# A four-layer graph network on one core: setup's weight products, the last group's transposes and the order of all steps are rewritten

## The chip, the core and the metric

The kernel runs on one core of a Trainium2 chip, in fp32 throughout. The metric is the time of one execution on the device in microseconds, the median of three runs. TensorE (PE) multiplies, VectorE (DVE), ScalarE (ACT) and GpSimd (POOL) do the element-wise work, and SyncE (SP) issues the DMAs.

## The reference

A batch of 128 elements, each with 128 nodes of 512 features, passes four layers that share one 128x128 adjacency matrix; each is followed by a residual and a layer norm.

```python
# layer 0: norm_adj = adj * rsqrt(deg) on both sides
x = LN(x + norm_adj @ (x @ W0) + bias)
# layer 1: W1 = W2 = adj, so C - A is the bias b and the maximum over the last axis stays elementwise
x = LN(x + max_m relu(A[n] + (C - A)[m]))
# layer 2
q, k, v = x @ Wq.T, x @ Wk.T, x @ Wv.T
rel = adj.T * (q @ k.T);  rel = rel / norm(rel, axis=2)
x = LN(x + rel @ v)
# layer 3
h = x @ W;  e = leaky_relu(h @ a1 [:, None] + h @ a2 [None, :]) * adj
x = LN(x + elu(softmax(e) @ h + beta * h))
```

## The kernel before

The batch is cut into 32 groups of four elements. A group passes a fixed chain of steps, and the chains of several groups overlap in time. A step's name has the group before the dot and the operation behind it (`4.z1`, `s.g0` for a step of setup).

The steps of a group, in the order of its data:
- `ld` loads x. `y` is norm_adj times x, which leaves x transposed. `w` is the product with W0 and `dw`, `uw`, `bi` add it and the bias to x (TensorE, then VectorE and POOL). `stw`, `vaw`, `pow`, `nbw`, `apw` are statistics, variance, power -1/2, shift and the normalising pass on ScalarE.
- `xt` and `xd` transpose x: VectorE transposes 32x32 squares into a tile `u`, of which there is one buffer, and sixteen DMAs on SyncE (L558) put the squares in place. `z` is x times Wq^T Wk, `v` is x times Wv^T, `r` is z times x transposed, one 128x128 block per element. `rm` multiplies by the adjacency, `sq` and `rp` make the norm, `rt`, `wr`, `cr` transpose the result (`relT`) by VectorE's squares and DMAs through DRAM. `f` is `relT` times v, `fa` adds it, and `stv` to `apv` normalise.
- `nt`, `nd` transpose again as `xt`, `xd` do. `k` is the product with W, `sc` makes the two row products s1, s2 (eight VectorE operations), `pw`, `pe` write s2 to DRAM and read it back spread over all partitions, `pl`, `ej`, `ei`, `ex`, `rd`, `so` are the leaky relu, the mask, the softmax and beta's diagonal, `at`, `aw`, `cat` transpose the attention (`attT`) through DRAM. `h` is attention times k, `em`, `ee`, `ea` are the elu with the residual, `stk` to `apk` normalise, `fin` stores.

The four large products w, z, v, k of a group are not computed as eight block products but as seven (class `Product`): both factors are cut in two by two blocks, sums of blocks are formed ahead (`sy`, `sx`, `sn` on POOL for the left factor, `w_sum`, L349, on VectorE for the weights), and seven products of four 256-wide matmuls each, numbered in the order `ORDER`, go to four PSUM banks. Product 6 accumulates onto the bank of product 1, 3 onto that of 5, 4 onto that of 7, each after the bank's first content was read:

```python
    ORDER = (1, 2, 5, 7, 6, 3, 4)
    ONTO = {6: 1, 3: 5, 4: 7}
```

For z, v and k the steps `c`, `d`, `t`, `u` copy and add the banks into a tile (ScalarE, VectorE, ScalarE, POOL). [...]

Setup computes, besides the normalised adjacency: Wq^T Wk in four row blocks of four 512-wide matmuls (`g`, L425) with copies on ScalarE (`cg`), Wv transposed by sixteen TensorE transposes (`t`, L440) with copies on ScalarE (`ct`), the sums of all weights (`s`, `sg`, `sv`), the products of W with a1 and a2 (`q`, eight VectorE operations), and eight TensorE transposes `wa` that spread these over all partitions.

Nothing is scheduled by a program at run time: the strings HEAD, TURN and TAIL list all steps, and each engine's queue holds its instructions in the order of that list. HEAD starts the first groups, TURN is repeated with one group more each time, TAIL ends. A step that waits holds up everything that is behind it on its engine. In TURN, TensorE's order is z of group g, f of g-1, r of g, w of g+1, y of g+2, v of g, h of g-2, k of g-1.

Of the kernel before, what the change touches and what calls it, by code (L numbers as in the profile page):

```python
# [37 lines left out]
F32 = mybir.dt.float32  # L38
# [6 lines left out]
TINY = 1.2e-38  # L45
GB = 4
# [15 lines left out]
s.t3 1.uw11 1.stw0 s.ct2 2.y10 s.ct3 1.stw1 2.y00 2.bi10 2.cy10 2.y11 2.cy00 s.sv0 2.y01 2.cy11
s.sv2 0.z1 s.sv1 2.cy01 s.sv3 1.stw2 0.sx0 0.z2 0.cz1 1.stw3 0.sx1 1.vaw 0.z5 0.dz2 0.sx2 0.z7
1.pow 0.cz5 0.sx3 0.z6 0.dz7 2.sy0 0.z3 0.tz 1.nbw 2.sy1 1.apw0 1.apw1 1.xt0 0.uz11 0.z4 1.apw2
0.dz3 2.sy2 1.xt1 1.apw3 0.r0 0.dz4 2.bi00 1.xt2 0.r1 1.xt3 0.r2 2.sy3 1.xd 0.r3 2.bi11 0.v1
0.rm 0.rt 0.sq0 2.bi01 0.sq1 0.v2 0.cv1 0.sq2 0.sq3 0.v5 0.rp 0.dv2 0.v7 0.cv5 0.v6 0.dv7 0.v3
0.tv 0.wr 0.uv11 0.v4 0.dv3 1.sx0 0.cr 3.y10 0.dv4 1.sx1 3.y00 3.cy10 3.y11 3.cy00 1.sx2 3.y01
3.cy11 3.sy1 3.w1 3.cy01 3.sy0 3.w2 3.dw1 1.sx3 3.w5 3.dw2 3.sy2 3.bi10 3.w7 3.dw5 3.sy3 3.w6
3.dw7 3.bi00 3.w3 3.bi11 3.tw 3.bi01 3.w4 3.uw10 3.dw3 0.f0 3.uw01 3.dw4 0.f1 0.fa0 3.uw11 0.f2
0.fa1 0.f3 0.stv0 1.z1 0.fa2 0.fa3 0.stv1 1.z2 1.cz1 0.stv2 0.stv3 1.z5 1.dz2 0.vav 3.stw0 0.pov  # L70
1.z7 1.cz5 3.stw1 0.nbv 1.z6 3.stw2 0.apv0 1.dz7 0.apv1 0.nt0 0.apv2 1.z3 3.stw3 1.tz 0.apv3
0.nt1 1.uz11 1.z4 1.dz3 0.nt2 0.nt3 2.w1 1.dz4 3.vaw 3.pow 2.w2 2.dw1 3.nbw 3.apw0 2.w5 2.dw2
3.apw1 3.apw2 2.w7 2.dw5 3.apw3 2.w6 2.dw7 2.w3 2.tw 2.uw01 2.w4 2.uw10 2.dw3 2.stw0 2.uw11 s.wa
0.nd 2.dw4 2.stw1 1.r0 2.stw2 2.stw3 1.r1 0.sc00 1.r2 2.vaw 1.r3 0.sc01 2.pow 0.sc10 1.v1 1.rm
2.nbw 1.sq0 1.rt 1.v2 1.cv1 0.sc11 2.apw0 0.sc20 2.apw1 1.v5 1.dv2 2.apw2 0.sc21 1.wr 2.apw3
1.v7 0.sc30 1.cv5 0.sc31 1.sq1 1.sq2 0.pw 1.v6 1.dv7 1.sq3 0.sn0 2.xt0 1.cr 2.xt1 1.v3 1.tv
0.sn1 2.xt2 2.xt3 0.sn2 1.v4 1.dv3 0.pe 1.uv11 0.k1 2.xd 1.dv4 0.sn3 0.k2 0.pl0 1.rp 0.ck1 0.pl1
0.pl2 0.k5 0.dk2 0.pl3 0.ej 0.ei 0.k7 0.ck5 0.ex0 0.ex1 0.k6 0.dk7 0.ex2 0.ex3 0.rd 0.so0 0.k3
0.tk 0.so1 0.so2 0.so3 0.uk11 0.at 0.k4 0.dk3 0.aw 1.f0 0.dk4 3.xt0 2.sx0 1.f1 1.fa0 0.cat 1.f2
2.sx1 3.xt1 1.f3 3.xt2 2.sx2 4.y10 3.xt3 1.fa1 4.y00 3.xd 4.cy10 4.bi10 1.fa2 4.y11 4.cy00 1.fa3  # L80
2.sx3 4.y01 4.cy11 1.stv0 2.z1 4.cy01 4.sy0 1.stv1 1.stv2 4.sy1 2.z2 2.cz1 1.stv3 4.sy2 1.vav
2.z5 2.dz2 1.pov 4.sy3 2.z7 2.cz5 1.nbv 4.bi00 1.apv0 2.z6 2.dz7 1.apv1 1.sc00 4.bi11 1.apv2
1.sc01 2.z3 2.tz 4.bi01 1.sc10 1.apv3 1.sc11 2.uz11 2.z4 2.dz3 1.nt0 3.sx0 2.r0 1.sc20 3.sx1
2.dz4 2.r1 1.nt1 2.r2 3.sx2 1.nt2 2.r3 1.nt3 3.sx3 2.v1 1.sc21 2.rm 1.sc30 2.sq0 2.v2 2.cv1 2.rt
2.sq1 1.sc31 2.wr 2.sq2 2.v5 2.sq3 2.dv2 1.pw 2.rp 2.v7 2.cv5 2.cr 2.v6 2.dv7 2.v3 1.pe 2.tv
2.uv11 2.v4 2.dv3 1.pl0 0.h0 1.nd 2.dv4 1.pl1 1.pl2 0.h1 0.em0 1.pl3 1.ej 0.h2 0.ee0 0.em1 0.h3
0.em2 0.ee1 3.z1 0.em3 0.ee2 0.ea0 0.ee3 0.ea1 3.z2 3.cz1 0.ea2 0.ea3 3.z5 0.stk0 0.stk1 3.z7
3.cz5 0.stk2 0.stk3 3.z6 3.dz7 0.vak 1.ei 0.pok 3.z3 3.tz 3.dz2 1.ex0 3.uz11 1.ex1 3.z4 1.ex2
0.nbk 3.dz3 1.sn0 0.apk0 0.apk1 0.fin0 4.w1 1.sn1 3.dz4 0.apk2 0.fin1 0.apk3 1.sn2 0.fin2 4.w2
4.dw1 1.ex3 0.fin3 1.sn3 1.rd 4.w5 1.so0 1.so1 1.so2 1.so3 4.w7 5.ld 4.dw5 1.at 4.dw2 1.aw 4.w6  # L90
4.dw7 4.w3 4.tw 4.uw01 1.cat 4.w4 4.uw10 4.dw3 4.stw0 4.uw11 2.f0 4.dw4 2.f1 2.fa0 4.stw1 2.f2
2.fa1 2.f3 2.fa2 1.k1 2.fa3 2.stv0 1.k2 1.ck1 2.stv1 2.stv2 1.k5 1.dk2 2.stv3 1.k7 1.ck5 4.stw2
2.vav 4.stw3 2.pov 1.k6 1.dk7 2.nbv 4.vaw 2.apv0 4.pow 1.k3 1.tk 2.nt0 2.apv1 1.uk11 1.k4 1.dk3
2.apv2 2.nt1 2.apv3 2.nt2 3.r0 1.dk4 3.r1 2.nt3 3.r2 4.nbw 2.nd 2.sc00 4.apw0 3.r3 2.sc01 4.apw1
1.h0 2.sc10 4.apw2 3.rm 1.h1 4.apw3 1.em0 3.sq0 1.h2 1.em1 3.sq1 1.h3 1.ee0 1.em2 1.ee1 3.v1
1.em3 1.ee2 3.rt 1.ee3 1.ea0 3.v2 3.sq2 1.ea1 3.cv1 3.sq3 1.ea2 3.rp 3.v5 1.ea3 1.stk0 3.wr
1.stk1 3.v7 3.cv5 1.stk2 1.stk3 3.v6 3.dv7 2.sn0 3.cr 4.xt0 3.v3 3.tv 2.sn1 1.vak 4.xt1 4.xt2
2.sn2 3.v4 4.xt3 3.dv2 1.pok 3.dv3 5.y10 4.xd 2.sn3 3.dv4 5.y00 5.cy10 1.nbk 5.y11 5.cy00 2.sc11
3.uv11 1.apk0 5.y01 2.sc20 5.sy1 1.apk1 2.sc21 2.k1 1.apk2 2.sc30 5.bi10 1.apk3 2.sc31 2.k2
2.ck1 5.bi00 5.cy01 5.cy11 2.k5 5.bi11 2.dk2 5.sy0 2.k7 2.ck5 5.bi01 1.fin0 2.k6 2.dk7 1.fin1  # L100
5.sy2 1.fin2 1.fin3 5.sy3 2.k3 2.tk 2.pw 4.sx0 2.k4 2.dk3 4.sx1 6.ld 4.z1 2.dk4 4.sx2 2.pe
2.uk11 4.z2 4.cz1 4.sx3 4.z5 4.dz2 2.pl0 2.pl1 2.pl2 4.z7 4.cz5 2.pl3 2.ej 4.z6 4.dz7 2.ei 4.z3
2.ex0 4.tz 2.ex1 4.uz11 4.z4 2.ex2 4.dz3 2.ex3 2.rd 2.so0 3.f0 4.dz4 3.f1 2.so1 3.fa0 3.f2 3.fa1
3.f3 3.fa2 4.r0 3.stv0 3.fa3 4.r1 3.stv1 4.r2 3.stv2 4.r3 3.stv3 5.w1 2.so2 3.vav 2.so3 4.rm
3.pov 5.w2 5.dw1 4.sq0 4.sq1 3.nbv 2.at 3.apv0 5.w5 5.dw2 2.aw 3.apv1 3.nt0 3.apv2 3.sc00 5.w7
3.apv3 5.dw5 4.sq2 3.nt1 4.sq3 2.cat 5.w6 5.dw7 4.rp 3.nt2 5.w3 3.nt3 5.tw 4.rt 5.uw01 3.nd
3.sc01 5.w4 5.uw10 5.dw3 3.sc10 5.uw11 6.y10 5.dw4 5.stw0 6.y00 6.cy10 6.bi10 5.stw1 6.y11
6.cy00 6.bi00 5.stw2 6.y01 6.cy11 5.stw3 4.v1 6.sy0 6.cy01 3.sc11 6.sy1 5.vaw 3.sc20 4.v2 4.cv1
3.sc21 5.pow 3.sc30 4.v5 6.sy2 4.wr 5.nbw 4.dv2 6.sy3 4.v7 5.apw0 3.sc31 4.cv5 6.bi11 5.apw1
5.xt0 3.pw 4.v6 4.dv7 5.apw2 4.cr 3.sn0 5.xt1 5.apw3 4.v3 5.xt2 4.tv 3.sn1 5.xt3 3.sn2 4.v4 3.pe  # L110
4.dv3 4.uv11 2.h0 5.xd 4.dv4 3.sn3 2.h1 2.em0 3.pl0 2.h2 2.em1 6.bi01 2.ee0 2.h3 2.ee1 2.em2
3.pl1 2.ea0 3.k1 2.ee2 2.em3 3.pl2 3.pl3 2.ea1 2.ee3 3.k2 2.ea2 3.ck1 2.ea3 2.stk0 3.k5 2.stk1
2.stk2 3.k7 3.ck5 2.stk3 3.ej 3.k6 2.vak 3.dk7 2.pok 3.ei 3.k3 3.tk 2.nbk 3.dk2 3.ex0 3.uk11
2.apk0 3.k4 3.dk3 2.apk1 5.sx0 2.fin0 2.apk2 2.fin1 5.sx1 5.z1 3.dk4 2.apk3 2.fin2 3.ex1 2.fin3
5.sx2 3.ex2 5.z2 5.cz1 5.sx3 3.ex3 3.rd 5.z5 5.dz2 7.ld 3.so0 3.so1 3.so2 5.z7 5.cz5 3.so3 3.at
3.aw 5.z6 5.dz7 5.z3 5.tz 5.uz11 3.cat 5.z4 5.dz3 4.f0 5.dz4 4.f1 4.fa0 4.f2 4.stv0 4.f3 4.fa1
4.fa2 5.r0 4.fa3 5.r1 4.stv1 5.r2 4.stv2 5.r3 4.stv3 6.w1 5.rm 4.vav 5.sq0 5.rt 4.pov 5.sq1 6.w2
6.dw1 5.wr 5.sq2 5.sq3 4.nbv 4.apv0 5.rp 6.w5 6.dw2 4.apv1 4.nt0 4.apv2 4.sc00 5.cr 6.w7 4.apv3
6.dw5 4.nt1 6.w6 6.dw7 4.nt2 4.nt3 6.w3 6.tw 4.sc01 4.nd 6.uw01 4.sc10 6.w4 6.uw10 4.sc11 6.dw3
6.uw11 7.y10 4.sc20 6.dw4 7.y00 7.cy10 7.bi10 6.stw0 7.y11 7.cy00 6.stw1 7.bi00 7.y01 7.cy11  # L120
6.stw2 5.v1 7.sy0 7.cy01 6.stw3 7.sy1 4.sc21 5.v2 5.cv1 6.vaw 4.sc30 6.pow 4.sc31 5.v5 7.sy2
# [58 lines left out]
TURN = """  # L180
# [87 lines left out]
def kernel(  # L268
# [116 lines left out]
    weights = {"0": (w0, w0_t), "g": (gq, gq_t), "v": (wvT, wvT_t), "3": (w3, w3_t)}  # L385
    W = {k: w_blocks(*v) for k, v in weights.items()}

    class Setup:


        def __init__(self):
# [12 lines left out]
        def root(self):  # L404
            nc.gpsimd.tensor_tensor(self.root_, self.safe, minus_half[:, 0:1], ALU.pow)
# [557 lines left out]
```

## Time and profile before

| | us |
|---|---|
| median of 3 runs | 2049.76 (2047.73 to 2051.08) |
| profiled execution | 2050.26 |
| its span, first to last instruction | 2048.5 |
| TensorE busy in the span | 2020.1 |
| VectorE busy | 1472.0 |
| POOL busy | 1006.9 |
| ScalarE busy | 771.8 |

Busy time is that of the profiled execution. The profiled execution took 1.8 us more than its span. A row such as `L595 PE MATMUL p_w<-w_t,S_y` names the line, the engine, the operation and the tiles; each fp32 matmul of 128x256 shows as two records. A matmul's record is longer than its distance to the next[...]: costs on TensorE are read from the starts of the records, not from their lengths.

### The profile page before, as it was taken

The page shows a single profiled execution, that of the slowest core. Times are in us where ns is not written, and L with a number is a line of the kernel's source. Part 1 is how long each engine was busy: PE and PEld are TensorE (multiplying, and loading weights), DVE is VectorE, ACT ScalarE, POOL GpSimd, SP SyncE. Part 2 cuts the span into 40 slices and gives each one's busy share as a digit, 9 for nine tenths or more (in the row PEclk, how much of TensorE's full clock was granted, in tenths as well). Part 3 has the DMA queues.
Part 4 walks back from the last instruction along what each step waited for, and adds up shares of the span by engine and source line. Part 5 has one row for each costly group of instructions (what it writes and reads, how often), then busy time and mean ns, then how long its engine had stood idle before and what let it go on. Part 6 is the DMA issues. An engine that isn't in the chain of part 4 may idle for free.

```text
span 2048.5 us, 29135 instructions
## 1 busy us (share of the span) xinstructions
PE 2020.1 (99%) x9786; PEld 1699.6 (83%) x9786; DVE 1472.0 (72%) x3048; ACT 771.8 (38%) x1609; POOL 1006.9 (49%) x840
## 2 busy tenths in 40 slices
PE   9999999999999999999999999999999999999996
PEld 6988888888888888888888888888888888888874
DVE  5477767677776777766776767777667767876876
ACT  2233334343333433343433334433334334332434
POOL 5735354554435555345545355554355452654432
PEclk9999999999999999999999999999999999999998
DMA  6224344433434433434434444334344333443533
GB/s 231 43 50 74 85 89 102 101 78 78 93 93 94 103 62 90 97 91 98 83 77 93 92 95 101 70 84 97 88 98 98 66 90 103 82 95 60 106 65 100
DMA packets 732980, 184.27 MB, mean 90 GB/s; under 512 B 684832, under 2 KB 684960, under 8 KB 732832
## 3 DMA queue, kind: packets, MB, share of 16 engines
q1 hardware_dynamic: 732832, 182.42, 41.2%
q8 instruction: 78, 1.28, 0.3%
q14 instruction: 70, 0.57, 0.1%
HBM read 64.82 MB, written 50.40 MB: 56 GB/s over the span
## 4 chain that ended last, share of the span: by engine, by line
PE 96%; SPq 1%; DVE 1%; issue 1%; DMA 1%; ACT 0%; POOL 0%; POOLq 0%; ACTq 0%; DVEq 0%
PE p_z L595 19%; PE p_w L595 19%; PE p_v L595 18%; PE p_k L595 17%; PE py L639 6%; PE pl_v L778 5%; PE pr L737 5%; PE pl_k L778 5%; SPq L558 1%; PE pg L425 1%; DVE prod L797 0%; SPq L572 0%; ACT x L699 0%; DMA s<-d_s 0%; DVE C_k L487 0%
## 5 line engine op out<-in xcount | busy, mean ns | idle before, releaser
L490 POOL TENSOR_TENSOR x<-x,t_w 128x512 f32<-128x512 f32 x96 | 119.5, 1273 | 158.5 <-ACT t_w L484 157.1
L487 DVE TENSOR_TENSOR x<-p_w,x 128x512 f32<-128x512 f32 x192 | 131.7, 687 | 81.0 <-PE p_w L595 66.8
L797 DVE SCALAR_TENSOR_TENSOR prod<-x,wa_bc 128x512 f32<-128x512 f32 x256 | 171.8, 671 | 4.6 <-ACT x L699 0.9
L595 PE MATMUL p_k<-w_t,S_n 128*128 128x256 f32 x768 | 171.5, 379 | 2.9 <-DVE C_k L487 1.9
L595 PE MATMUL p_w<-w_t,S_y 128*128 128x256 f32 x768 | 171.0, 379 | 0.0
L595 PE MATMUL p_z<-S_x,gq_t 128*128 128x256 f32 x768 | 171.0, 379 | 0.0
L595 PE MATMUL p_v<-wvT_t,S_x 128*128 128x256 f32 x768 | 171.0, 379 | 0.0
L490 POOL TENSOR_TENSOR x<-x,bias_bc 128x512 f32<-128x512 f32 x128 | 162.1, 1278 | 15.6 <-PE py L639 13.7
L595 PEld LDWEIGHTS p_k<-w_t,S_n 128*128 128x128 f32 x768 | 145.7, 190 | 23.8 <-DVE C_k L487 2.7
L595 PEld LDWEIGHTS p_w<-w_t,S_y 128*128 128x128 f32 x768 | 145.9, 190 | 19.8
L595 PEld LDWEIGHTS p_z<-S_x,gq_t 128*128 128x128 f32 x768 | 145.9, 190 | 19.8
L595 PEld LDWEIGHTS p_v<-wvT_t,S_x 128*128 128x128 f32 x768 | 145.9, 190 | 19.8
L494 POOL TENSOR_TENSOR r_v<-v,minus_half 128x4 f32<-128x4 f32 x32 | 32.9, 1029 | 255.9 <-DVE v L686 247.8
L753 ACT ACTIVATE sq<-rel 128x128 f32<-128x128 f32 x128 | 39.6, 309 | 267.0 <-DVE rel L487 264.3
L494 POOL TENSOR_TENSOR r_k<-v,minus_half 128x4 f32<-128x4 f32 x32 | 32.5, 1016 | 214.0 <-DVE v L686 211.4
L639 PEld LDWEIGHTS py<-nadjT,x 128*128 128x128 f32 x1024 | 121.5, 195 | 4.1 <-issue 1.4
L639 PE MATMUL py<-nadjT,x 128*128 128x128 f32 x1024 | 121.9, 278 | 0.4 <-DVE nadjT L418 0.4
L699 ACT ACTIVATE x<-x,nb,r_w 128x512 f32<-128x512 f32 x128 | 96.9, 808 | 66.8 <-DVE nb L693 62.2
L778 PE MATMUL pl_k<-C_k,attT 128*128 128x512 f32 x256 | 116.8, 599 | 3.7 <-DVE C_k L487 3.0
L778 PE MATMUL pl_v<-C_v,relT 128*128 128x512 f32 x256 | 116.7, 599 | 2.8 <-DMA relT<-d_r 2.8
L490 POOL TENSOR_TENSOR C_z<-C_z,t_z 128x512 f32<-128x512 f32 x32 | 40.6, 1270 | 160.2 <-ACT t_z L484 160.2
L487 DVE TENSOR_TENSOR C_z<-p_z,t_z 128x512 f32<-128x512 f32 x64 | 44.1, 688 | 91.2 <-PE p_z L595 88.2
(991 smaller groups left out, 4644.5 us busy)
## 6 DMA issues: line engine op xcount, KB each, us to landing
out_dram<-x SPq DMA_DIRECT2D x128, 256.0 KB, 2.1
x<-in_x_dram SPq DMA_DIRECT2D x31, 1024.0 KB, 5.4
d_r<-ru SPq DMA_DIRECT2D x32, 256.0 KB, 2.0
relT<-d_r SPq DMA_DIRECT2D x128, 64.0 KB, 2.6
s<-d_s SPq DMA_DIRECT2D x32, 256.0 KB, 4.0
d_a<-au SPq DMA_DIRECT2D x32, 256.0 KB, 2.3
attT<-d_a SPq DMA_DIRECT2D x128, 64.0 KB, 2.6
x<-in_x_dram SPq DMA_DIRECT2D x2, 512.0 KB, 4.2
```

Source lines behind the costliest of these rows:

```text
L425: nc.tensor.matmul(wide(pg), lhsT=wq_sb[:, ec, bass.ts(gc, P)], rhs=wk_sb[:, ec, :], start=(ec == 0), stop=(ec == KC - 1),)
L487: nc.vector.tensor_tensor(o, a, b, f)
L490: nc.gpsimd.tensor_tensor(o, a, b, f)
L494: nc.gpsimd.tensor_tensor(r, v, minus_half, ALU.pow)
L558: nc.sync.dma_start(out=self.aT[rows(to), :, :, rows(q)], in_=self.u[rows(q), :, :, to])
L595: nc.tensor.matmul(ps[:, j, :], lhsT=lhsT, rhs=rhs, start=(i not in ONTO and j == 0 and kc == 0), stop=(j == 1 and kc == 1), skip_group_ch ...
L639: nc.tensor.matmul(o, lhsT=self.x_chunk(b, kc), rhs=nadjT, start=True, stop=True)
L699: nc.scalar.activation(xt, xt, AF.Identity, bias=self.nb[k][:, b : b + 1], scale=self.rstd[k][:, b : b + 1],)
L737: nc.tensor.matmul(self.pr[:, b, :], lhsT=self.whole["z"][:, fc, b // 2, bass.ts(b % 2, P)], rhs=self.xT.chunk(b, fc), start=(fc == 0), st ...
L753: nc.scalar.activation(scratch, self.rel[:, b, :], AF.Square, accum_out=self.n2[:, b : b + 1])
L778: nc.tensor.matmul(ps, lhsT=left[:, b, :], rhs=self.whole[k][:, b, :], start=True, stop=True)
L797: nc.vector.scalar_tensor_tensor(prod, self.x[:, b, :], 1.0, wide(wa_bc[k]), ALU.mult, ALU.mult, accum_out=self.s[:, k, b : b + 1],)
```

## The change

Setup's Wq^T Wk is computed as the groups' products are, by seven block products: Wq's block sums on POOL (`sa`), Wk's on VectorE (`sk`), the banks emptied by `cg`, `dg`, `tg`, `ug`. Wv is transposed by four VectorE transposes (`vt`) and sixteen DMAs (`vd`) instead of on TensorE. Seven transposes of the identity are issued on TensorE ahead of all else (`warm`). In the last group (group 31) the three transposes that went through DMAs (`rt`, `pe`, `at`) are TensorE transposes with a copy (or, for s2, with the ScalarE step reading PSUM directly), k is a plain product of four 512-wide matmuls per element, and its k, elu, statistics and power go by single batch elements, interleaved with h. HEAD and TAIL are new lists, TURN has the same steps in another order; TURN now starts at group 6 instead of 10 and is repeated 16 times instead of 17, and TAIL is longer. The methods `t_`, `c_first`, `c_add`, `c_last` of the groups move into `Product` unchanged in what they do.

```diff
+WARM = 7
-FIRST = 10
-LAST = -5
+FIRST = 6
+LAST = -10
...
+        def exchange(self, o):
+            for q in range(4):
+                for to in range(4):
+                    nc.sync.dma_start(out=o[rows(to), :, :, rows(q)], in_=self.u[rows(q), :, :, to])
...
+    class Columns(Left):
+        def __init__(self, name, w):
+            self.name, self.w = name, w
+            self.s = big.tile([P, 4, 2, HD], F32, tag="S", name=f"S_{name}")
+        def block(self, p, h):
+            return self.w[:, 2 * h : 2 * h + 2, p * HD : (p + 1) * HD]
...
-        def g(self, gc):
-            self.banks["g", gc] = pg = bank(f"pg_{gc}")
-            for ec in range(KC):
-                nc.tensor.matmul(
-                    wide(pg),
-                    lhsT=wq_sb[:, ec, bass.ts(gc, P)],
-                    rhs=wk_sb[:, ec, :],
-                    start=(ec == 0),
-                    stop=(ec == KC - 1),
-                )
-        def t(self, dc):
-            self.banks["v", dc] = pv = bank(f"pwv_{dc}")
-            for ec in range(KC):
-                nc.tensor.transpose(pv[:, ec, :], wv_sb[:, ec, bass.ts(dc, P)], ident)
...
+            self.wq = Columns("wq", wq_sb)
+            self.wv = Squares("wv")
+            self.po = Product("g", self.wq, "k")
+        def warm(self):
+            pt = bank("pt_warm")
+            for _ in range(WARM):
+                nc.tensor.transpose(pt[:, 0, :], ident, ident)
+        def sa(self, i):
+            self.wq.sum(i)
+        def vt(self, i):
+            self.wv.square(i, wv_sb[:, i, :])
+        def vd(self):
+            self.wv.exchange(wvT.rearrange("p k (c e) -> p k c e", c=KC))
...
+            self.end = g == NG - 1
+        def k_plain(self, b):
+            self.pk = self.pk if b else {}
+            self.pk[b] = psum.tile([P, D], F32, tag="bank", name=f"pk_{b}")
+            for kc in range(KC):
+                nc.tensor.matmul(self.pk[b], lhsT=self.nT.chunk(b, kc), rhs=w3[:, kc, :],
+                                 start=(kc == 0), stop=(kc == KC - 1))
+        def c_plain(self, b):
+            copy(self.whole["k"][:, b, :], self.pk[b])
+        def transpose(self, name, t):
+            ps = bank(name)
+            for b in range(GB):
+                nc.tensor.transpose(ps[:, b, :], t(b), ident)
+            return ps
...
         def cr(self):
+            if self.end:
+                self.relT = mid.tile([P, GB, P], F32, tag="relT", name="relT_end")
+                copy(self.relT, self.prt)
+                return
...
         def pe(self):
+            if self.end:
+                s2 = lambda b: self.s[:, 1, b : b + 1].to_broadcast([P, P])
+                self.s2 = self.transpose("ps2", s2).rearrange("p b j -> p j b")
+                return
```

The part of HEAD in which setup's new steps meet group 1's product, and the end of TAIL (13 is group 31 there):

```
s.g4 s.q10 s.q11 s.q12 s.q13 s.bi 0.bi01 s.wa 2.ld 3.ld 4.ld s.s31 2.y10 s.s33 0.uw01 2.y00 2.cy10
2.cy00 s.sv0 0.stw0 0.uw10 0.stw1 0.uw11 s.sv2 s.tg 0.stw2 2.sy1 2.y11 0.stw3 2.y01 2.cy11 s.ug11
s.dg3 2.cy01 0.vaw 1.y10 2.sy0 s.dg4 1.y00 1.cy10 s.sg0 1.y11 1.cy00 s.sg2 1.y01 s.sg1 1.cy11 s.sg3
1.w1 1.cy01 s.sv1 s.sv3 1.w2 1.dw1 1.sy0 1.sy1 1.w5 1.dw2 1.sy2 1.w7 1.dw5 0.pow 1.sy3 1.w6 1.dw7
...
13.em0 12.nbk 13.ee0 12.apk0 13.ea0 12.apk1 13.stk0 12.fin0 12.apk2 12.fin1 13.vak0 13.h1
13.pok0 13.ck2 12.fin2 13.k3 13.em1 12.apk3 13.nbk0 13.ee1 12.fin3 13.apk0 13.ea1 13.stk1
13.fin0 13.vak1 13.h2 13.pok1 13.ck3 13.h3 13.em2 13.nbk1 13.ee2 13.em3 13.apk1 13.ea2 13.ee3
13.fin1 13.stk2 13.ea3 13.vak2 13.stk3 13.pok2 13.vak3 13.pok3 13.nbk2 13.nbk3 13.apk2 13.apk3
13.fin2 13.fin3
```

## The prediction

> **What bounds the kernel now.** I read the page's busy shares first, then the table by stage, then what TensorE waited for, then the timelines of the first 110 and the last 100 us.
>
> ```profile
> PE 2020.1 (99%) x9786; PEld 1699.6 (83%) x9786; DVE 1472.0 (72%) x3048; ACT 771.8 (38%) x1609; POOL 1006.9 (49%) x840
> ```
> ```profile
> 0.00:20.00 20.00, 14.99 (x73) 13.64 (x74) 8.03 (x15) 3.62 (x5) 10.09 (x15) 1.00 0.91 325
> ...
> 800.00:1000.00 200.00, 200.00 (x989) 170.05 (x988) 146.11 (x308) 78.51 (x160) 106.84 (x89) 1.00 0.43 89
> ...
> 1950.00:2000.00 50.00, 46.07 (x206) 36.68 (x205) 37.62 (x87) 17.93 (x49) 15.56 (x13) 0.97 0.38 66
> ...
> 2010.00:2020.00 10.00, 7.04 (x18) 3.77 (x17) 5.75 (x13) 5.02 (x15) 1.60 (x2) 0.83 0.18 65
> ...
> 2040.00:2048.50 8.50, 0.00 (x0) 0.00 (x0) 1.27 (x5) 2.93 (x4) 1.01 (x1) 0.50 0.33 123
> ```
> ```profile
> PE pt_nadj L414 <- DVE nadj L410: 4.6, 1, 4.6
> PE pl_k L778 <- DVE C_k L487: 3.0, 1, 3.0
> PE pl_v L778 <- DMA relT<-d_r: 2.8, 1, 2.8
> PE p_k L595 <- DVE C_k L487: 1.9, 2, 1.1
> PE p_k L595 <- DVE x L880: 1.0, 1, 1.0
> PE pl_k L778 <- DMA attT<-d_a: 0.8, 1, 0.8
> ```
>
> TensorE is full for 1950 us: a group takes 62.36 us (y_10T's first copy at 552.7, y_15T's at 864.5), and products z, w, v, k (12.09 each, as 1942.77 to 1954.86), y and r (3.57 each), f and h (3.43 each) add up to the same 62.36. A new order of the other engines can win nothing there, and loses only if it makes TensorE wait. The reader is to see in the rows by stage (TensorE's busy time first, the granted clock as third number from the end) that the first 20 us miss 5.0 and the last 100 about 25, and in the list of waits that the last 80 us have six different causes of 1 to 3 us each: no single one is worth much, they have to go together. What can be won lies outside: 5.0 us before product y, its slow first records, 9.5 us of waits in the last 80 us, half speed after two of them, and the 13.9 us from the last matmul (2034.6) to the end.
>
> **The change, part by part.** *TensorE's work.* Wq^T Wk in seven blocks: 13.73 us (23.72 to 37.45) become one product's 12.09: -1.64. Wv's sixteen transposes stand 0.11 apart (53.1 to 54.8): -1.75. In the last group k is plain, sixteen 512-wide matmuls, which is 13.73 for 12.09: +1.64; twelve transposes add 1.31.
>
> *The warm-up.* Seven transposes run before L414, in time that TensorE waits anyway (4.6 us), so they cost nothing; were identity late they could delay L414 by at most their 7 x 0.24.
>
> ```profile
> L639 PE MATMUL py<-nadjT,x x4: 421/421/582, 5.7 to 6.5; 128*128 128x128 f32 x4
> L639 PE MATMUL py<-nadjT,x x6: 275/275/275, 11.0 to 11.5; 128*128 128x128 f32 x6
> ```
>
> The first y records start 0.21 us apart, from about 10.3 us on 0.11: y takes 5.96 (5.67 to 11.63) instead of 3.57, so up to 2.4 is there to be won. [...] the two transposes at 4.56 and the y records behind them did not open the clock until 10.3, though the seven would end near 3.1 and leave a gap besides. I take 0.3.
>
> *Setup's new queue.* The order of steps puts, on VectorE behind group 0's last add (24.7 us, 24.9 with Wk's sums before it): four transposes of Wv (0.63 apart, to 27.5), then sums and the eight row products of W3 (0.735 each), done near 37.0. TensorE ends Wq^T Wk at 35.8 and waits for those with its `wa` transposes: +0.4. SyncE then issues sixteen exchange DMAs. The same pattern is in the trace:
>
> ```profile
> 45.11 11.54 SPq L558 DMA_DIRECT2D x_0T<-sq_x  x16
> ```
> ```profile
> 41.40 1.75 DVE L349 TENSOR_TENSOR gq_t<-gq,gq_t 128x512 f32<-128x512 f32 x1
> ...
> 55.60 2.34 DVE L349 TENSOR_TENSOR wvT_t<-wvT 128x512 f32<-128x512 f32 x2
> 57.86 2.35 DVE L349 TENSOR_TENSOR wvT_t<-wvT,wvT_t 128x512 f32<-128x512 f32 x2
> ```
>
> From 45.11 to POOL's first use of x_0T (58.35) are 13.2 us, so wvT is there at 40.7. Of the loads on SyncE, those of groups 3 and 4 move behind the exchange (to about 40); group 3's is used by its y at 70, so that costs nothing; were it used at once, it would cost its landing time of 5.4 us. The four sums of Wq on POOL (1.27 each) come between S_y's before 25 us; they push the bias adds back into POOL's idle stretch, the 10 us before 40.1; without that stretch group 0's statistics would come 5 us later. The four copies of Wv that ScalarE loses were off the path. VectorE's order has the first Wv sum ahead of group 0's statistics, two adds of Wq^T Wk, four sums of it, the other Wv sums, and then group 1's first add. VectorE thus stands for wvT from 38.5 to 40.7, and what is queued behind it is group 1's add, for which TensorE's fifth w product waits (it accumulates onto the first one's bank). TensorE comes there at 37.2 + 7.15 (two y) + 6.91 (four products) = 51.3. VectorE's list is eight sums, four statistics pairs (0.80), three adds (0.64) and a small one. Unhindered (0.6 a sum) it ends at 50.9: no wait. The rows above show sums beside POOL at 1.15 each (4.62 for four): then 55.5, a wait of 4.2. POOL has S_y of two groups, eight operations of 1.27, in just this time, so I take 3.0. A wait of that length can also halve the clock: after the waits of 2.8 and 3.0 in the tail pl_v took 5.18 for 3.60 and four pl_k records 3.41 for 1.8, with a granted clock of 0.83 in that row. That is 1.6 each; I take half, 0.8. The setup is then -1.64 - 1.75 + 0.4 + 3.0 + 0.8 - 0.3 = +0.5. Ends: -5.5 (all hidden, clock opened) and +3.
>
> *The last stage.* Counted from the last group's r. Before: 1954.86 to 2048.5 is 93.6 us, of which 65.65 are TensorE's work. After, with 0.2 for a hand-over: r and v to 15.7; transposes to 16.1; ScalarE's copy of relT (0.59) takes the place of the DMA's wait of 2.8: f from 17.05 to 20.5; k of group 29 to 32.6. Behind f VectorE adds and takes statistics, ScalarE applies, and eight row products (0.735) end at 34.1; their transposes and the add behind them let h of 29 start at 34.85: a wait of 1.8. It ends at 38.3. In k of group 30 the third product needs a bank that h of 29 holds until the first L880-type add, which stands behind four transposes, four L873-type adds, two operations on e and one on C_k, at 43.2: a wait of 1.55. So k ends at 51.95, h at 55.4, the transposes at 55.9 (the attention's DMA and its 0.8 are gone; VectorE's copy hides), then four k products and four h (17.15) at 73.05. Then add, exp, add, statistics, power (1.0), two applies and the output: 0.9 + 0.6 + 0.7 + 0.9 + 1.3 + 0.3 + 1.6, and the 3.1 from last apply to end (2045.4 to 2048.5), at 83.0 with the gaps between: 10 instead of 13.9. That the last group's statistics, powers and applies go one batch element at a time is what makes this end shorter: only the last element's chain stands behind the last matmul, where now four adds, four exps, four adds and four statistics do (2034.7 to 2041.0). The twelve DMAs that the last group no longer issues free SyncE early; n_31T, issued from 38.7, lands 13.2 later at 52, before its first use at 55.9. The stage gains 93.6 - 83.0 = 10.6, its added work included, and no wait in it is long enough to halve the clock. VectorE has some 63 us of work in the 83; each hand-over that is 0.2 longer costs up to 3 in all, and a late x_31T or n_31T more. Ends: 7 and 12.
>
> Sum: 2048.5 + 0.5 - 10.6 = 2038.4. Around the span lie 1.76 us (2050.26 - 2048.5); the profiled execution is 0.5 above the median of 2049.76. So 2038.4 + 1.76 - 0.5 = 2039.7.
>
> **The rivals.** *A, as worked out:* 2037 to 2043.5, chance 0.60. *B, setup's wait is hidden:* sums fall between POOL's operations; for it speaks that of the eleven such sums from 34 us on eight took 0.66 to 0.69, against it that the three that began while POOL ran took 1.64 to 1.76, and POOL will be running. Without 3.8, and with the clock opened, 2033.5 to 2037: 0.22. *C, the tail gives less or setup's wait is longer:* VectorE is nearly as loaded as TensorE at the end (63 of 68 us), so a slip of a few us in its queue moves h and k; half of the tail's gain, 5, makes 2043.5 to 2048: 0.14. *D, slower:* in the turns the transposes `xt` of the next group overwrite the tile that the sixteen DMAs of n read; VectorE waited 1.8 us for them at 936.5, and now all four stand ahead of the last two adds of v, which free banks for h. Those had 0.4 us of slack at 939.99 (VectorE's idle time before them). If n landed d later than now, each of sixteen turns would lose d - 0.4; the gain of 10 is eaten and 0.2% lost from d = 1.3 on (16 x 0.9 = 14): 2054 and more, 0.04. Against it: SyncE's queue ahead of n holds the same DMAs, and its sources are written at the same place. *E, the warm-up does nothing:* likely, and worth 0.3 in A.
>
> **The numbers.** About 0.2%, 4 us, is what a measurement of this kernel can tell from no change. Faster by more means under 2045.7: A, B and half of C, 0.89; within: 0.07; slower 0.04. The range leaves out the ends of B and C: 2033.0 to 2046.0.
>
> **What would show it.** Right: TensorE busy throughout the turns at 62.36 a group; a wait of TensorE for VectorE's add in p_w near 51 us, with VectorE waiting for the wvT DMAs near 40; y still at 0.21 between records; the end some 10 us after the last matmul; no wait on relT or attT DMAs in the last group. Wrong: no idle TensorE between 6 and 150 us (B), y at 0.11 from the start, a wait that repeats each turn (D), or over 8 us of waits after the last r (C).

## The result, and the profile after

The changed kernel took 2038.95 us, the median of 4 runs (2038.5 to 2041.29), against 2049.95 for the kernel before (4 runs, 2047.73 to 2051.08): a ratio of 0.995, 95% interval 0.9933 to 0.9967. The forecast was 2039.7. The profiled execution took 2038.5 us with a span of 2036.7. Below are its busy shares, rows of its table by stage (columns as before: TensorE's busy time first, the granted clock third from the end), and all that TensorE waited for (us in total, times, longest).

```profile
PE 2019.5 (99%) x9789; PEld 1700.1 (83%) x9789; DVE 1551.9 (76%) x3061; ACT 768.1 (38%) x1606; POOL 1016.4 (50%) x843
```
```profile
0.00:20.00 20.00, 16.91 (x86) 14.97 (x87) 11.96 (x18) 4.22 (x6) 11.66 (x15) 1.00 0.93 321
20.00:40.00 20.00, 17.51 (x80) 14.35 (x79) 19.12 (x31) 1.17 (x2) 12.75 (x9) 0.97 0.81 211
40.00:60.00 20.00, 20.00 (x119) 18.44 (x119) 18.70 (x27) 7.03 (x12) 15.78 (x12) 0.94 0.24 89
800.00:1000.00 200.00, 200.00 (x989) 170.04 (x988) 153.94 (x306) 77.88 (x160) 107.22 (x90) 1.00 0.43 89
...
2010.00:2020.00 10.00, 10.00 (x27) 4.62 (x26) 7.66 (x18) 5.29 (x10) 1.01 (x1) 1.00 0.29 106
```
```profile
PE wa_bc L653 <- DVE wprod L638: 2.1, 5, 0.4
PE pt_warm L612 <- POOL ident masks.py:199: 1.4, 1, 1.4
PE pt_nadj L601 <- DVE nadj L597: 1.3, 1, 1.3
PE ps L808 <- DVE prod L885: 1.2, 1, 1.2
PE p_k L540 <- DVE C_k L419: 0.9, 1, 0.9
PE pl_v L866 <- ACT relT_end L416: 0.7, 1, 0.7
PE py L702 <- DVE nadjT L605: 0.4, 1, 0.4
PE p_g L540 <- DVE gq L419: 0.4, 1, 0.4
PE pl_k L866 <- DVE C_k L419: 0.3, 1, 0.3
```

Between 800 and 1000 us nothing moved on TensorE. The hole is now at 20 to 40 us: TensorE busy for 17.51 of 20 us, and the clock below 1 there and after. Before, it had been full there:

```profile
20.00:40.00 20.00, 20.00 (x73) 11.88 (x73) 14.65 (x36) 4.07 (x8) 7.07 (x6) 1.00 0.65 243
```

At the end the long waits of 2.8 and 3.0 us are gone, and with them the granted clock of 0.83 in the row from 2010 us. To split the time, take the start of the last group's r as the mark: 1955.11 us, against 1954.86 before, so everything ahead of it nets +0.25. From there to the last matmul's end (less the last 0.15 us of its record, in both) and from that to the end of the span, first after, then before:

```profile
1955.11:2027.90 72.79, 69.77 (x277) 48.56 (x275) 59.10 (x131) 33.94 (x75) 19.62 (x18) 1.00 0.39 91
2027.90:2036.70 8.80, 0.16 (x1) 0.00 (x0) 4.04 (x12) 3.35 (x5) 1.08 (x2) 0.75 0.24 89
```
```profile
1954.86:2034.50 79.64, 70.14 (x289) 52.79 (x287) 59.60 (x130) 30.62 (x76) 20.17 (x17) 0.96 0.38 81
2034.50:2048.50 14.00, 0.15 (x1) 0.00 (x0) 6.50 (x16) 4.48 (x8) 1.01 (x1) 0.63 0.28 106
```

The last stage fell from 93.64 to 81.59 us: 6.85 up to the last matmul, 5.20 behind it. The whole gain of 12 us is there. In the setup, less TensorE work was paid for with new waits.

### The profile page after: what moved, and what is told of

Same layout as the page of the kernel before. It is cut to its first block, busy times and chain, and to the rows that moved or that the text cites. A ratio compares the mean times of both kernels' runs of the same rounds, so it can differ in the third digit from the quotient of the medians.

```text
span 2036.7 us, 29180 instructions
## 1 busy us (share of the span) xinstructions
PE 2019.5 (99%) x9789; PEld 1700.1 (83%) x9789; DVE 1551.9 (76%) x3061; ACT 768.1 (38%) x1606; POOL 1016.4 (50%) x843
## 4 chain that ended last, share of the span: by engine, by line
PE 98%; DVE 1%; issue 0%; ACT 0%; DMA 0%; POOL 0%; DVEq 0%; POOLq 0%
PE p_w L540 19%; PE p_v L540 19%; PE p_z L540 19%; PE p_k L540 18%; PE py L702 6%; PE pr L817 6%; PE pl_k L866 5%; PE pl_v L866 5%; PE pk L792 1%; DVE wprod L638 0%; DVE prod L885 0%; PE p_g L540 0%; DVE w_t L371 0%; DVE C_k L419 0%; DMA adj_sb<-in_adj_dram 0%
## 5 line engine op out<-in xcount | busy, mean ns | idle before, releaser
L425 POOL TENSOR_TENSOR r<-v,minus_half 128x4 f32<-128x4 f32 (+1 forms) x99 | 100.0, 1010 | 507.8 <-DVE v L748 478.4
L762 ACT ACTIVATE x<-x,nb,r 128x512 f32<-128x512 f32 x384 | 283.9, 804 | 92.6 <-DVE nb L756 80.4
L540 PE MATMUL p_k<-w_t,S_n 128*128 128x256 f32 x744 | 165.7, 379 | 0.9 <-DVE C_k L419 0.9
L540 PEld LDWEIGHTS p_k<-w_t,S_n 128*128 128x128 f32 x744 | 141.3, 190 | 20.4 <-DVE C_k L419 1.3
L942 DVE SCALAR_TENSOR_TENSOR e<-e,rden,beta_i 128x128 f32<-128x128 f32 x128 | 113.5, 942 | 0.9
L975 ACT ACTIVATE pl_k<-pl_k 128x512 f32<-128x512 f32 x128 | 74.2, 582 | 105.1 <-DVE x L972 101.1
L866 PE MATMUL pl_k<-C_k,attT 128*128 128x512 f32 x248 | 111.6, 592 | 0.3 <-DVE C_k L419 0.3
L866 PE MATMUL pl_v<-C_v,relT 128*128 128x512 f32 x248 | 111.5, 592 | 0.0
```

The lines of the kernel that those rows point to most:

```text
L425: nc.gpsimd.tensor_tensor(o, v, minus_half[:, : v.shape[-1]], ALU.pow)
L540: nc.tensor.matmul(ps[:, j, :], lhsT=lhsT, rhs=rhs, start=(i not in ONTO and j == 0 and kc == 0), stop=(j == 1 and kc == 1), skip_group_ch ...
L762: nc.scalar.activation(xt, xt, AF.Identity, bias=self.nb[k][:, b : b + 1], scale=self.rstd[k][:, b : b + 1],)
L866: nc.tensor.matmul(ps, lhsT=left[:, b, :], rhs=self.whole[k][:, b, :], start=True, stop=True)
L942: nc.vector.scalar_tensor_tensor(self.e[:, b, :], self.e[:, b, :], self.rden[:, b : b + 1], beta_i, ALU.mult, ALU.add)
L975: nc.scalar.activation(self.pz[b], self.pz[b], AF.Exp)
```

## The experiments

Line numbers of the experiments' profiles differ by a few from those of the changed kernel. Medians, of 4 to 13 runs, are compared with the changed kernel's 2038.95. The kernel before, timed again beside each batch of experiments, had medians of 2049.91 to 2050.51, so differences of half a us say nothing.

**One half alone.** All steps in the changed order up to group 16's first z product; from there every step still to do in the order of before, and the last group as it was. Beside the lists of steps, one line differs:

```diff
-            self.end = g == NG - 1
+            self.end = False
```

> The changed kernel's order up to group 16's z, from there the order of the kernel before, with the last group's transposes through DMAs and k by seven products. If the setup's savings (3.4 us) and its waits cancel, as the start of the last r says (1955.1 against 1954.9 us), this is the time before, 2050 (2048.5 to 2051). If the setup alone gave a gain that the start of r hides, 2046 to 2047.

Measured: 2050.63 us, ratio to before 1.0002 (0.9994 to 1.001). So the new setup is worth nothing as it stands, and the gain belongs to the last stage. Two explanations of "nothing" had to be told apart: that its parts are too small, or that they are eaten.

**What ate the setup's gain.** In the changed kernel's queue of VectorE (start and length; SCALAR_TENSOR_TENSOR is the row product q), then in POOL's:

```profile
29.42 1.75 DVE L638 SCALAR_TENSOR_TENSOR wprod<-w,a_bc 128x512 f32<-128x512 f32 x1
...
36.23 0.69 DVE L638 SCALAR_TENSOR_TENSOR wprod<-w,a_bc 128x512 f32<-128x512 f32 x1
```
```profile
26.00 4.62 POOL L422 TENSOR_TENSOR x<-x,bias_bc 128x512 f32<-128x512 f32 x3
30.70 4.94 POOL L422 TENSOR_TENSOR x<-x,t_w 128x512 f32<-128x512 f32 x3
```

The four that begin while POOL adds (to 35.6 us) take 1.14 to 1.75 us, the four behind them 0.69. DMAs are not the difference: their share is 0.65 from 33.4 to 36.2 us and 0.66 from 36.2 to 39.1. In the kernel before, the same eight instructions all took 0.68 to 0.69, from 28.4 to 34.2 us. POOL had no addition there, only one 128x4 operation, and stood idle for 10.09 us up to 40.1:

```profile
28.44 0.68 DVE L451 SCALAR_TENSOR_TENSOR wprod<-w,a_bc 128x512 f32<-128x512 f32 x1
```
```profile
40.10 2.50 POOL L490 TENSOR_TENSOR S_y<-y_1T 128x512 f32<-128x512 f32 x2 [10.09 <-ACT y_1T L484]
```

The groups' row products show what else matters (shortest, median and longest in ns; first setup's eight, then the groups' 256):

```profile
L638 DVE SCALAR_TENSOR_TENSOR wprod<-w,a_bc x8: 691/916/1754, 29.4 to 38.4; 128x512 f32<-128x512 f32 x8
```
```profile
L885 DVE SCALAR_TENSOR_TENSOR prod<-x,wa_bc x256: 641/677/689, 127.6 to 1988.7; 128x512 f32<-128x512 f32 x128
```

The groups' all lie within 0.05 us (0.641 to 0.689), though 166 of them began while POOL ran. They are the same operation on the same shape, but read `wa_bc` from PSUM; setup's products read both inputs from SBUF, and the four beside POOL took 1.14 to 1.75. The traces show this difference, not what lies behind it. Nor is it setup's products alone: the softmax's 128 operations `e<-e,rden,beta_i`, with both inputs in SBUF, went from 0.39 to 0.94 us on average, since the new order of the turns puts 97 of them beside POOL instead of 13 (those clear of POOL take 0.32 to 0.35 in both kernels). That is 70 of the 80 us by which VectorE's busy time grew. It cost nothing: the list of TensorE's waits has none of them.

TensorE waits for setup's products with the `wa` transposes, and ahead of them with the last part of Wq^T Wk for an add that stands behind two products:

```profile
22.57 3.62 PE L540 MATMUL p_g<-wk_sb,wq_sb 128*128 128x256 f32 x16
...
39.46 8.69 PE L702 MATMUL py<-nadjT,x 128*128 128x128 f32 x64
47.99 3.62 PE L540 MATMUL p_w<-w,y_1T 128*128 128x256 f32 x16
51.44 5.40 PE L540 MATMUL p_w<-w_t,S_y 128*128 128x256 f32 x24
```

From the first record of Wq^T Wk (22.57) to group 2's y (39.46) it needs 16.9 us for 13.0 us of work, 0.6 of the loss at the last part of Wq^T Wk and 3.3 at `wa`. Then the clock halves for one step (granted 0.50 from 38.94 to 42.36; y's records stand 0.21 us apart there, 0.11 behind it), so that two y take 8.5 instead of 7.15: 3.9 + 1.4 = 5.3 us.

The first cure was to move q, wa and the load of group 4 away:

```diff
-s.q00 s.g6 s.q01 s.dg7 0.bi11 s.g3 s.q02 s.q03 s.g4 s.q10 s.q11 s.q12 s.q13 s.bi 0.bi01 s.wa 2.ld 3.ld 4.ld
+s.g6 s.dg7 0.bi11 s.g3 s.g4 s.bi 0.bi01 2.ld 3.ld
...
-1.z1 2.xd 0.dv4 1.z2 1.cz1 1.z5 1.dz2 1.z7 1.cz5 1.z6 1.dz7
+1.z1 s.q00 2.xd 0.dv4 1.z2 s.q01 1.cz1 s.q02 1.z5 s.q03 1.dz2 s.q10 1.z7 s.q11 1.cz5 s.q12 1.z6 s.q13 4.ld 1.dz7
...
-0.f0 1.dz4
+0.f0 s.wa 1.dz4
```

> The eight row products of W3 with a1 and a2 (q), their transposes (wa) and the load of group 4 (which needs the buffer that q frees) move from 29-39 us to 105-125 us, where VectorE and POOL have idle time. My reading is that TensorE's 3.7 us of waits for wprod at 33 to 39 us, and the 1.1 us of half clock behind them, came from VectorE instructions slowed by POOL (1.63 to 1.75 us each for four of the eight, 0.69 for the other four), and that nothing else waits there. Then both go: 4.8 us less, about 2034, no wait of TensorE between 6 and 1970 us. Rival: the second wait that I had forecast, group 1's add behind the sums of Wv and Wq^T Wk, appears near 51 us as soon as TensorE comes there in time, 1 to 3 us: then 2035 to 2037.

Measured: 2043.54 us, 4.6 more than the changed kernel. Both expectations had the sign wrong. The eight products took 0.68 to 0.69 each in their new place, and the wait at `wa` was gone, but the forecast's own wait came up, twice as long as in the rival's worst case. First what TensorE waited for, then its timeline, then VectorE's (in brackets the idle time before, and its cause):

```profile
PE p_w L538 <- DVE x L417: 6.5, 1, 6.5
```
```profile
56.72 3.75 PE L538 MATMUL p_w<-w_t,S_y 128*128 128x256 f32 x8 [6.48 <-DVE x L417]
```
```profile
39.96 1.76 DVE L369 TENSOR_TENSOR wvT_t<-wvT 128x512 f32<-128x512 f32 x1 [5.60 <-DMA wvT<-sq_wv]
...
47.87 2.38 DVE L369 TENSOR_TENSOR gq_t<-gq 128x512 f32<-128x512 f32 x2
50.17 3.41 DVE L369 TENSOR_TENSOR gq_t<-gq,gq_t 128x512 f32<-128x512 f32 x2
53.50 2.47 DVE L369 TENSOR_TENSOR wvT_t<-wvT,wvT_t 128x512 f32<-128x512 f32 x2
55.89 2.87 DVE L417 TENSOR_TENSOR x<-p_w,x 128x512 f32<-128x512 f32 x4
```

VectorE, now early, stands for the exchange of Wv until 39.96 with group 1's adds behind it, then makes sums beside POOL (5.8 us for four of Wq^T Wk), and reaches the add only at 55.9; TensorE had come at 50.1. Behind the wait of 6.5 us the clock was at half for two steps (55.6 to 62.4; the eight records of p_w above take 3.75, against 1.89 at full clock). In the changed kernel the products had filled VectorE's wait for the DMAs, and TensorE came almost 5 us later (54.9, behind two of the three parts that begin at 51.44 above). By then the first of these adds was just done:

```profile
54.05 2.87 DVE L419 TENSOR_TENSOR x<-p_w,x 128x512 f32<-128x512 f32 x4
```

One wait was the cover of the other.

So the sums of Wv had to go as well (the edit is against the run with q moved):

```diff
-2.cy10 2.cy00 s.sv0 0.stw0 0.uw10 0.stw1 0.uw11 s.sv2 s.tg
+2.cy10 2.cy00 0.stw0 0.uw10 0.stw1 0.uw11 s.tg
...
-1.cy01 s.sv1 s.sv3 1.w2
+1.cy01 1.w2
...
-1.nbw 0.sx1
+1.nbw s.sv0 s.sv2 0.sx1
...
-1.xt2 1.apw3 0.sx3 2.stw0
+1.xt2 s.sv1 1.apw3 0.sx3 2.stw0 s.sv3
```

> As the run with q moved, and the four sums of the transposed Wv (sv) also move, from their place in front of group 1's adds to 73-82 us, 10 us before product v of group 0 needs them. If the order of VectorE's queue is the whole cause (its first Wv sum waits for the exchange DMAs of Wv until 40 us, and group 1's add stands behind it and behind the slowed sums of Wq^T Wk), TensorE does not wait between 6 and 1970 us: the time is 4 to 5 us below the changed kernel, 2034 to 2035. If the sums of Wq^T Wk alone, at 1.7 us each beside POOL, hold the add, a wait of 1 to 3 us near 50 us stays and the time is 2036 to 2038. If TensorE's waits came from the DMAs of setup as such, the time is that of the run with q moved, 2043.5.

Measured: 2033.93 us, 5.0 less than the changed kernel; ratio to before 0.9922 (0.991 to 0.9934). TensorE's timeline has no gap left there, and group 1's w goes through without a stop:

```profile
35.85 7.31 PE L700 MATMUL py<-nadjT,x 128*128 128x128 f32 x64
43.00 3.62 PE L538 MATMUL p_w<-w,y_1T 128*128 128x256 f32 x16
46.45 5.34 PE L538 MATMUL p_w<-w_t,S_y 128*128 128x256 f32 x24
51.63 1.89 PE L538 MATMUL p_w<-w,S_y 128*128 128x256 f32 x8
```

The sums of Wq^T Wk still stood ahead of the add, beside POOL (6.3 us for four). What is gone from in front of it is the wait for the DMAs (5.6) and the Wv sums themselves (5.9): the add now begins at 46.5, and TensorE comes for it at 49.9. With the sums kept in their place it would have begun 1 to 3 us too late, by an estimate from these figures; that was not run.

**The warm-up.** Three runs: without it, with thirteen transposes, and with ordinary matmuls.

```diff
-s.warm s.deg s.root
+s.deg s.root
```

> The seven transposes of the identity ahead of all else are taken out, nothing else. In the changed kernel's profile the clock opened at 8.2 us, in the one before at 10.5, and y of group 0 took 4.9 us instead of 6.0. If the transposes opened the clock earlier: y takes 5.6 to 6.0 again and the time is about 1.0 us above that of the changed kernel, near 2040. [...]

```diff
-WARM = 7
+WARM = 13
```

> Thirteen transposes of the identity instead of seven, so that TensorE is busy from 1.4 us until nadj is there at 4.4. If transposes count as busy: the clock opens by 4.8 to 7, y takes 3.6 to 4.3, and the time falls by about 1 us to 2038. If they do not: no change, and y as in the changed kernel or in the one without a warm-up.

```diff
-                nc.tensor.transpose(pt[:, 0, :], ident, ident)
+                nc.tensor.matmul(pt[:, 0, :], lhsT=ident, rhs=ident, start=True, stop=True)
```

> The seven transposes become seven ordinary fp32 matmuls of the identity (two records each, 0.21 apart at half speed: 3.0 us, 1.4 to 4.4). If ordinary matmuls alone count: the clock opens by 4.8 to 7, y takes 3.6 to 4.3, the time falls by 0.7 to 1.4 us to about 2038. If the clock opens only after a fixed time of y itself: no change. If matmuls and transposes count alike, this run and the one with thirteen transposes open the clock equally early.

Measured: 2039.45, 2039.2 and 2038.32 us, all inside each other's spread (2037.46 to 2040.43). The warm-up does nothing that these runs can tell. TensorE starts at half speed (y's records stand 0.21 us apart, and 0.11 behind the opening), and the clock's opening is seen where y's records change length, here in the changed kernel:

```profile
L702 PE MATMUL py<-nadjT,x x12: 364/421/582, 5.5 to 8.0; 128*128 128x128 f32 x12
...
L702 PE MATMUL py<-nadjT,x x21: 274/275/364, 8.0 to 10.4; 128*128 128x128 f32 x21
```

The times below are those of the trace's first record of the granted clock. (It holds none from before the opening, so the tables by stage show 1.00 for the first 20 us.)

| kernel | y starts | clock opens | later by | y takes |
|---|---|---|---|---|
| before, no warm-up | 5.67 | 10.50 | 4.83 | 5.96 |
| changed, 7 transposes | 5.54 | 8.22 | 2.69 | 4.94 |
| without warm-up | 5.69 | 8.75 | 3.06 | 5.12 |
| 13 transposes | 5.61 | 9.95 | 4.35 | 5.73 |
| 7 matmuls | 5.70 | 9.50 | 3.80 | 5.47 |
| q moved, 7 transposes | 5.47 | 11.18 | 5.71 | 6.38 |

With the same seven transposes the delay runs from 2.69 to 5.71, and without any it was 4.83 in the kernel before and 3.06 in the run without a warm-up. Within one trace the clock changes only at multiples of 3.413 us from each other: in the changed kernel at 8.22, 38.94 and 42.36 (9 and 10 of them behind the first), in the kernel before at 10.50, 1973.17, 1976.58, 2014.13 and 2017.54 (575, 576, 587 and 588). Where the first of these points falls differs from run to run, and with nearly the same start (5.54 and 5.47) y takes 4.94 or 6.38.

What TensorE did ahead of these points does not settle what opens the clock. In the changed kernel the 3.41 us up to the opening (4.81 to 8.22) held 2.69 us of y and 0.28 of transposes. In three other runs the clock was still at half behind the 3.41 us that end one step ahead of the opening. With q moved (4.35 to 7.76) they were filled just as long, with 2.29 us of y and 0.68 of transposes; with thirteen transposes (3.13 to 6.54) they held 0.93 of y and 1.96 of transposes; with matmuls in their place (2.67 to 6.08) 2.42 us of matmuls and 0.54 of transposes. Whether transposes weigh in it as y does, these four stretches do not show, nor whether matmuls would help in another run.

**The last stage, one part undone at a time.** First the statistics: the last group's variance, power, shift and applies over the whole group again.

```diff
-13.fin0 13.vak1 13.h2 13.pok1 13.ck3 13.h3
+13.h2 13.ck3 13.h3
...
-13.fin1 13.stk2 13.ea3 13.vak2 13.stk3 13.pok2 13.vak3 13.pok3 13.nbk2 13.nbk3 13.apk2 13.apk3 13.fin2 13.fin3
+13.stk2 13.ea3 13.stk3 13.vak 13.pok 13.nbk 13.apk0 13.fin0 13.apk1 13.fin1 13.apk2 13.fin2 13.apk3 13.fin3
```

> In the last group the final variance, power, shift and the four normalising passes go over the whole group again, behind the last statistics; all else as in the changed kernel. From the changed kernel's trace: the statistics of the last element end 4.9 us before the end; then come variance 0.2, power 1.0 (0.54 for one element), shift 0.2, four passes (3.0 instead of 0.8 for the last) and the same 3.0 to the end. That is 2.6 us more, about 2041.5. If the store and not this chain set the end, nothing changes.

Measured: 2042.02, 3.1 more. ScalarE's last row, first here, then in the changed kernel:

```profile
2034.30 2.93 ACT L757 ACTIVATE x<-x,nb,r 128x512 f32<-128x512 f32 x4 [3.91 <-DVE nb L751]
```
```profile
2032.14 1.56 ACT L762 ACTIVATE x<-x,nb,r 128x512 f32<-128x512 f32 x2 [2.42 <-DVE nb L756]
```

Four passes behind the last power instead of one and a half. (The profile shows 3.6 us more than that of the changed kernel; y took longer in it.) Second, the plain k: seven products again.

```diff
-            elif self.end and kind == "k":
-                self.k_plain(*n)
-            elif self.end and kind == "ck":
-                self.c_plain(*n)
...
+13.k6 13.dk7 12.nbk 12.apk0 12.apk1 12.fin0 13.k3 13.tk 12.apk2 12.fin1 13.uk11 13.k4 13.dk3
+12.fin2 12.apk3 12.fin3 13.h0 13.dk4 13.h1 13.em0 13.h2 13.ee0 13.em1 13.h3
```

> The last group's k goes by seven block products again, with h of all four elements behind it; the statistics still go by single elements. TensorE's work is 1.64 us less. Against that, h waits for the last add (0.3 to 0.9), the third product for the first sum on POOL (about 1.0 in the kernel before), and four elements instead of two stand in the chain behind the last matmul (2.5 us more). I expect 1.5 to 3 us more than the changed kernel, 2040.5 to 2042. If the plain k bought nothing, it is 1 to 1.6 us less, 2037.5.

Measured: 2041.8, 2.9 more. TensorE ends its last matmul at 2027.67, 0.23 earlier, of the 1.64 us that it saves: 0.85 is lost in front of h, and the last group's r began 0.55 later, 0.24 of it from y. Behind it stand 12.0 us (to 2039.7) instead of 8.8, with h of all four elements at the end. Third, relT by DMAs: VectorE's squares behind group 30's leaky relu (their tile is free only then), then one DMA out and four in, as in the other groups:

```diff
-            if self.end:
-                self.prt = self.transpose("prt", lambda b: self.rel[:, b, :])
-                return
             self.ru = self.square("ru", self.rel)
...
-10.pok 12.pl3 13.v7
+10.pok 12.pl3 13.rt 13.wr 13.v7
...
-10.fin1 12.ej
+10.fin1 13.cr 12.ej
```

> In the last group relT alone is transposed through DRAM again (VectorE squares, one DMA out, four in) instead of by four transposes and a copy; all else as in the changed kernel. The squares need the tile that s2 of group 30 leaves only after its leaky relu, near 1965 us, and from the squares to relT the kernel before took some 7 us. So f should wait 2 to 3 us for the DMAs (2.8 before) instead of 0.84, and half the clock afterwards (1.6): 2041 to 2043. If the order of the queues alone removed the wait, relT is there in time and the 1.3 us of transposes and hand-over are saved: 2037.5.

Measured: 2043.24, 4.3 more, as expected and a little over:

```profile
1975.05 5.37 PE L861 MATMUL pl_v<-C_v,relT 128*128 128x512 f32 x8 [2.89 <-DMA relT<-d_r]
```

A wait of 2.89 us, and f in 5.4 instead of 3.7 behind it. Of the last stage's 12 us these three parts carry 3.1 + 2.9 + 4.3 = 10.3, if they add up; attT and s2 were not undone alone.

**A version that beats both.** The setup of the run with q and sums moved, and the waits left in the last stage taken away by order alone: relT's transposes ahead of the third part of v, s2's behind group 30's third product, x of group 31 sent earlier.

```diff
-13.v6 12.nt3 10.apk1 10.fin0 13.dv7
+13.v6 13.rt 12.nt3 10.apk1 10.fin0 13.dv7 13.cr 13.v3
...
-13.rt 12.nd 13.dv4 13.cr 12.rd 12.so0
+12.nd 13.dv4
...
-12.sn3 11.dk3 13.pe 13.pl0 11.dk4 11.h0
+13.nt2 11.k3 13.nt3 13.nd 12.sn1 11.tk 11.k4 11.dk3 11.uk11 12.sn2 13.sc10 13.sc11 11.dk4 11.h0
...
+12.k5 12.dk2 11.ea2 13.pe 13.pl0
```

> The kernel with q and the sums moved (2033.9), and the last stage reordered: the last group's relT transposes go between the sixth and the last two parts of v; its x is transposed and sent ahead of the row products, in front of attT of group 30 on SyncE; the transposes of s1 and s2 come after the third product of group 30's k; the elu of group 29 comes ahead of group 31's mask. This takes the three waits that are left in the last stage (0.84 before f, 1.09 before s2, 1.02 in group 30's k: 2.9 us) if nothing new is late: 2031. If VectorE, busy for 63 of some 66 us, only moves its lag on to the last h or to the chain behind the last matmul, 2032 to 2034.

Measured: 2034.12, no gain on 2033.93. The rival held: the three waits were gone (by the starts of the records 3.8 us and not 2.9: the one at s2, with its second half in front of h, is 1.93), and two others stood in front of h of groups 29 and 30 (1.2 and 2.1 us), whose adds were behind the moved work on VectorE. Once more, with the adds first:

```diff
-11.k3 13.nt3 13.nd 12.sn1 11.tk 11.k4 11.dk3 11.uk11
+11.k3 11.tk 11.uk11 12.sn0 11.k4 11.dk3 13.nt0 13.nt1 12.sn1 11.dk4 13.nt2 13.nt3
...
-13.rd 13.so0 13.so1 13.so2 13.so3 11.stk2 12.k4 12.dk3
+12.k4 12.dk3 11.stk1 12.h0 12.dk4 12.h1 13.rd 13.so0 13.so1
```

> The last reordered stage once more. In the run before, TensorE waited 1.2 us and 2.1 us in front of the h of groups 29 and 30 for adds on VectorE, which stood behind the last group's transposes (these waited 1.3 us for the DMAs that still read their tile) and behind its statistics and softmax. Now the adds of k come ahead of both, the softmax's transposes on TensorE come behind the first part of the last k, and attT of group 30 goes ahead of n of group 31 on SyncE. If these two places were all, the 3.2 us fall away: 2031. If VectorE is simply full, the lag appears in front of another product or at the last h, and the time stays at 2033 to 2034.

Measured: 2031.7 us (2030.86 to 2033.19), ratio to before 0.991 (0.9894 to 0.9927), 7.3 less than the changed kernel. Of that, 5.0 is the setup; the 2.2 from the new order of the end are at the edge of the spread (the run with the sums moved had 2033.16 to 2034.55). One wait is left behind the start:

```profile
PE pl_k L860 <- ACT C_k_end L410: 1.4, 1, 1.4
```

## Why the prediction was right, point by point

- *Sum.* 2038.4 of span was forecast, 2036.7 measured. The setup gave +0.25 for +0.5, the last stage 12.05 for 10.6. The last stage was right in its mechanism. The setup was right only in its sum.
- *The setup's wait, the step that failed.* The prediction had TensorE waiting 0.4 at `wa` and 3.0 near 51 us, with 0.8 of half clock. The time went 3.9 at `wa` and just ahead of it, with 1.4 of half clock, and nothing at 51. The term that failed is "the eight row products of W3 (0.735 each), done near 37.0". The price was right for the kernel before, where just these instructions stood in POOL's idle stretch. But the change fills that stretch: the same paragraph has the bias adds pushed into it. The slowdown beside POOL, used there for the sums (1.15), was not used for the products; four took 1.14 to 1.75, and they were done at 39.1. TensorE then came to group 1's fifth product at 54.9, when VectorE had just done the add that it began at 54.05. The wait at 51 was real, as the run with q moved showed with 6.5 us; only its cover was not seen.
- *Luck in it.* That waits and half clock came out near the forecast (5.3 for 4.2) is luck in part: one wait stood in for another. Most of what was over was made up by y, 1.0 shorter in this profile for 0.3 forecast. With the 3.4 us of saved work the parts come to about +0.75, and half a us of the measured +0.25 is not placed.
- *The warm-up.* 0.3 was taken, y became 1.0 shorter. As far as the runs show it was not the transposes: without them y took 5.96 and 5.12, with the same seven 4.94 and 6.38. It goes with where the clock opened, 2.69 to 5.71 us behind y's start; what sets that point was not shown.
- *The last stage.* The stations, counted from r, forecast and measured: f at 17.05 and 16.93, h of group 29 at 34.85 and 34.92, the last k at 55.9 and 55.54, the last matmul's end at 73.05 and 72.95. The waits were 0.84, 1.93 and 1.02 for 0.9, 1.8 and 1.55, and the granted clock stayed at 1.00 from r to the last matmul. The end took 8.6 for 10: the power of one element took 0.54 instead of 1.0, and only one apply (0.8) of the two was behind the last shift.
- *The rivals.* B (setup's wait hidden) is what the sums-moved run is, and its 2033.5 to 2037 held 2033.93. B had other grounds, though: sums that fall between POOL's operations, not sums moved away. D had its place in the turns, and none of them has a wait. E, the warm-up does nothing, is what the three runs say within their spread.
- *A reading.* In the kernel before, the last 100 us miss 23.4 us of TensorE by the table, where the prediction says about 25; nothing hangs on it.

## What to carry to other kernels

A queue with two waits in it can hide the second behind the first: before taking one away, ask who then arrives early and what is queued there. The price of an instruction holds for what ran beside it: setup's row products cost 0.69 us in POOL's idle stretch, and up to 1.75 when the new order put POOL's adds there. Where the operands lay made the difference in these traces: the groups' products, with one input in PSUM, stayed at 0.64 to 0.69. Where one engine is full in the middle, gains lie in the start and the end; in the end, count the chain behind the last matmul by single elements.

## What the runs showed of the hardware that was not expected

The clock also halved behind stretches that were not all idle. In the kernel before, the stretch ahead of f held the last 0.98 us of product v, then the wait for relT, and behind it the clock was at 0.50 for one step:

```profile
1969.70:1973.10 3.40, 0.98 (x5) 0.53 (x3) 1.25 (x2) 0.00 (x0) 3.40 (x3) 1.00 0.55 99
1973.20:1976.50 3.30, 2.97 (x4) 1.45 (x5) 0.77 (x2) 0.00 (x0) 1.38 (x2) 0.50 0.33 77
```

Waits of 1.08 and 0.99 us in the k of group 30 of the same kernel left it at 1.00. In the changed kernel, the stretch from 35.5 to 38.9 us held transposes for half its time (1.62 us of records), and the clock halved as well:

```profile
35.50:38.90 3.40, 1.62 (x8) 0.62 (x5) 3.26 (x9) 0.00 (x0) 0.14 (x1) 1.00 0.69 86
38.95:42.35 3.40, 3.16 (x15) 3.16 (x16) 3.33 (x9) 0.59 (x1) 0.00 (x0) 0.50 0.96 364
```

These records are transposes alone; what other matmuls for half of the time would have done, the traces do not show. Behind five waits of 0.4 us between single transposes, half clock thus cost 1.4 us, behind the one wait of 2.9 us in the run with relT by DMAs 1.7.
